# First attention of a Perceiver block: where the projection stands in TensorE's queue, a 28th ring slot, and who shifts the last scores

## The chip, the cores and the metric

The kernel runs on one core of one Trainium2 chip. The metric is device time in microseconds (us) of one execution, and the figure given is the median of several executions. Everything is fp32. The engines of the core are TensorE (PE in the profile, with PEld for its weight loads), VectorE (DVE), ScalarE (ACT), GpSimd (POOL) and SyncE (SP, which only issues transfers here). The program gives each engine its own queue of instructions.

## The reference

The model has two blocks. Each does cross-attention of 128 rows of x (256 wide) on a long context of 12,544 rows (192 wide), then self-attention, then a feed-forward part with experts. Only the first cross-attention is touched by the diff, apart from the size of a buffer ring that all stages share:

```python
q = (x @ Wq + bq).reshape(B, N, 16, 16)
k = (y @ Wk + bk).reshape(B, M, 16, 16)      # M = 12544
v = (y @ Wv + bv).reshape(B, M, 16, 16)
scores = jnp.einsum('bnhd,bmhd->bhnm', q, k) / sqrt(16)
attn = softmax(scores, axis=-1)
out = jnp.einsum('bhnm,bmhd->bnhd', attn, v)
h = relu(out @ W1 + b1)
x = x + (h @ W2 + b2)
```

The softmax runs over 12,544 keys, for 16 heads and 128 queries. The kernel does not hold all scores at once, so it works with maxima of parts of the keys and corrects for them at the end.

## The kernel before, in words

**Tiling.** The first attention handles the heads in two octets of eight. Within an octet it goes through the context in superblocks of 1024 keys (the last has 256), and a superblock is cut into groups of 256 keys. There are 49 groups per octet, 98 in all, and one step `t` of the main loop begins with one group. Ten groups in a row (or nine at the end of an octet) form a range. A range has its own maximum per query and head. There are ten ranges, which start at steps 0, 10, 20, 30, 40, 49, 59, 69, 79 and 89.

**A group's life.** `scores(t)` (TensorE, L411) writes the scores of a group into two PSUM tiles of two banks each, one for each k in 0, 1. `keep(t)` copies both tiles to two slots of an SBUF ring (ScalarE, L424) and folds them into a running maximum `mx` of the range (VectorE, L429). The copy of one tile goes on while the maximum of the other is taken. The pool has two buffers of that kind, so the next scores need both tiles to have been copied and compared. When the range has ended, `fold` halves `mx` (L436), `range_maximum` turns it with TensorE transposes (L250) and reduces it on VectorE (L446), and one step later `range_spread` spreads the negated maximum over all partitions with further transposes (L255) into two PSUM banks, one of the `w` kind and the bank `m`. `range_spread_out` copies them to SBUF (ScalarE, L466). Twelve steps after its scores, a group's slots get that value added: three quarters by GpSimd from SBUF (`shifted_gpsimd`) and one quarter by VectorE from the PSUM bank (`shifted_vector`), both on L476; from group 86 on it is half and half. Then ScalarE takes the exponentials (L486). One step later `attend` multiplies with v on TensorE (L499) into one bank `o` per range. At the end of the range `collected` and `gather` move the result to `accs`.

**The projection.** Keys and values are projected from the context on TensorE four steps ahead (`pieces(t + AHEAD)`, `AHEAD` is 4). A superblock has four pieces: the first half of the keys, the second half of the keys, the first half of the values and the second half of the values. A first half does the part of the contraction that is laid out in two row tiles (L214 for keys, L232 for values), for both of its PSUM banks, and then the whole part for the first bank (L217, L239). A second half does the whole part of the second bank. VectorE evacuates each bank (`keys_out` L372, `values_out` L376). Keys go to one of three `kT` buffers, values to one of `NV = 5` buffers `vs`. The first piece also issues the context loads for its superblock on SP (L198, L200).

**Buffers.** The ring has `RING = 27` slots of 128 x 1024. The first attention holds two slots per group for `LAG = 13` steps. The later stages use the same ring for weights and for the second attention's scores. [...]

**Order.** The order on every engine is written out by hand in a loop of `len(groups) + LAG + 1` steps, under `tc.manual_schedule()`. Within a step t, with `o = t - LAG` and `e = t - LAG + 1`, it goes: scores of t, spread, `attend(o)`, GpSimd's shifts of e, `keep(t)`, spread out, exponentials of e, VectorE's shifts of e + 1, fold and range maximum, collecting, the projection pieces, gathering.

**The second attention** has a similar loop of its own (scores L786, p*v L860, projection L214 to L239), and its copies to the ring are on L803, its sums on L883. Its order is not part of the diff.

Of the kernel before, what the change touches and what calls it, by code (L numbers as in the profile page):

```python
# [8 lines left out]
F32 = mybir.dt.float32  # L9
AF = mybir.ActivationFunctionType  # L10
ALU = mybir.AluOpType
AX = mybir.AxisListType

P = 128
# [4 lines left out]
NE = 8  # L19
KB = 512  # L20
SB = 1024
RING = 27
EPS = 1e-5


# [8 lines left out]
def perceiver(ctx: ExitStack, tc: tile.TileContext, a: dict, out: bass.AP):  # L34
    nc = tc.nc
# [17 lines left out]
    def ps_w(name):  # L53
        return banks["pool"].tile([P, KB], F32, tag="w", name=name, bufs=banks["w"])
# [36 lines left out]
    ident = const.tile([P, P], F32, name="ident")  # L91
# [154 lines left out]
    def turned(pt, src):  # L246

        m = src.shape[1]
        for i in range(m):
            nc.tensor.transpose(pt[:, i * P : (i + 1) * P], src[:, i, :], ident)  # L250
        return pt[:, : m * P].rearrange("p (m q) -> p m q", q=P)
# [52 lines left out]
    with tc.tile_pool(name="l0w", bufs=1) as lw:  # L304
# [4 lines left out]
        with psum_pool("ps0", 2) as pp, tc.tile_pool(name="l0x", bufs=1) as work:  # L309
# [3 lines left out]
            AHEAD, LAG = 4, 13  # L313
            NV = 5
# [5 lines left out]
            range_of, start_of = [], []  # L320
# [3 lines left out]
                range_of.append(len(start_of) - 1)  # L324
            last_of = [t for t in range(len(groups)) if last[t]]

            kTs, ps, mx, folded, spreads, kept, os, deferred = {}, {}, {}, {}, {}, {}, {}, {}
            vs = [work.tile([P, 8, 152], F32, name=f"x0_v{i}") for i in range(NV)]
            for v in vs:
                nc.gpsimd.memset(v, 1.0)  # L330
# [86 lines left out]
            def keep(t, st):  # L417

                b = range_of[t]
                ps[t] = [slot(f"x0_p{t}_{k}") for k in range(2)]  # L420
                if t == start_of[b] + 1:
                    mx[b] = work.tile([P, 2, 2, KB], F32, tag="mx", name=f"x0_mx{b}")
                for k in range(2):
                    nc.scalar.copy(ps[t][k], st[k].rearrange("p a n -> p (a n)"))  # L424
                    if first[t]:
                        continue
                    m = mx[b][:, 1 - k]
                    old = ps[t - 1][1 - k].rearrange("p (a n) -> p a n", a=2) if t == start_of[b] + 1 else m
                    nc.vector.tensor_tensor(m, st[1 - k], old, ALU.max)  # L429

            def fold(b):

                folded[b] = work.tile([P, 2, 2, 256], F32, tag="folded", name=f"x0_folded{b}")
                for k in (1, 0):
                    m = mx[b][:, k].rearrange("p a (c n) -> p a c n", c=2)
                    nc.vector.tensor_tensor(folded[b][:, k], m[:, :, 0], m[:, :, 1], ALU.max)  # L436

            def bank_m(name):
                return pp.tile([P, KB], F32, tag="m", name=name, bufs=1)

            def range_maximum(b):
                free = last_of[b] - LAG + 4 >= start_of[b]
                for k in (1, 0):
                    pt = bank_m(f"x0_mt{b}_1") if k and free else ps_w(f"x0_mt{b}_{k}")
                    pt = turned(pt, folded[b][:, k].rearrange("p a (u q) -> p (a u) q", q=P))
                    nc.vector.tensor_reduce(  # L446
                        negmax[:, b].rearrange("p (u i) -> p i u", u=2)[:, 2 * k : 2 * k + 2],
                        pt.rearrange("p (a u) q -> p a u q", u=2), AX.X, ALU.max, negate=True,
                    )

            def range_spread(b):

                pbs = [x.rearrange("p (a n) -> p a n", a=2) for x in (ps_w(f"x0_mb{b}"), bank_m(f"x0_m{b}"))]
                kept[b] = pbs[1]
                for k in range(2):
                    for i in range(2):
                        for u in range(2):
                            h = 4 * u + 2 * k + i
                            spread_column(pbs[k][:, i, u * P : (u + 1) * P], negmax[:, b, h : h + 1])
                return pbs  # L460
# [6 lines left out]

            def shares(t):

                return (2, 1) if t + LAG - 1 < len(groups) else (2, 0)  # L470

            def shift(engine, t, k, banks, by):
                if banks.stop > banks.start:
                    v = ps[t][k].rearrange("p (a c n) -> p a c n", a=2, c=2)[:, banks]
                    n = banks.stop - banks.start
                    engine.tensor_tensor(v, v, by[:, banks].unsqueeze(2).to_broadcast([P, n, 2, 256]), ALU.add)  # L476
# [3 lines left out]
                    shift(nc.gpsimd, t, k, slice(0, shares(t)[k]), spreads[range_of[t]][:, 2 * k :])  # L480

            def shifted_vector(t):
                shift(nc.vector, t, 1, slice(shares(t)[1], 2), kept[range_of[t]])

            def exponent(t, k):
                nc.scalar.activation(ps[t][k], ps[t][k], AF.Exp)  # L486
# [20 lines left out]
            def collected(b):  # L507
                oT = work.tile([P, 2, P], F32, tag="oT", name=f"x0_oT{b}", bufs=1)
                nc.vector.tensor_copy(oT.rearrange("p u q -> p (u q)"), os.pop(b)[:, 0:256])
                return oT  # L510

            def gather(b, oT):

                pt = turned(ps_w(f"x0_ot{b}"), oT)
                nc.vector.tensor_copy(
                    accs[:, b].rearrange("p (u i) d -> p u i d", u=2),
                    pt.rearrange("p u (i d) -> p u i d", i=4)[:, :, :, 0:17],
                )

            with tc.manual_schedule():  # L520
                for t in range(AHEAD):
                    for f in pieces(t):
                        f()
                oTs = {}
                for t in range(len(groups) + LAG + 1):
                    e, o = t - LAG + 1, t - LAG
                    e = e if 0 <= e < len(groups) else None
                    o = o if 0 <= o < len(groups) else None
                    st = scores(t) if t < len(groups) else None
                    b = range_of[t - 2] if 2 <= t < len(groups) + 2 and last[t - 2] else None  # L530
                    spread = range_spread(b) if b is not None else None
                    if o is not None:
                        attend(o)
                    if e is not None:
                        shifted_gpsimd(e)
                        if first[e]:
                            shifted_vector(e)
                    if t < len(groups):
                        keep(t, st)
                    if b is not None:  # L540
                        range_spread_out(b, spread)
                    if e is not None:
                        for k in range(2):
                            exponent(e, k)
                    if 0 <= t - LAG + 2 < len(groups) and not first[t - LAG + 2]:
                        shifted_vector(t - LAG + 2)
                    if 1 <= t < len(groups) + 1 and last[t - 1]:
                        fold(range_of[t - 1])
                        range_maximum(range_of[t - 1])
                    if o is not None and last[o]:  # L550
                        oTs[range_of[o]] = collected(range_of[o])
                    for f in pieces(t + AHEAD):
                        f()
                    if t > LAG and last[t - LAG - 1]:
                        b = range_of[t - LAG - 1]
                        gather(b, oTs.pop(b))

                nr = NR // 2
                acc = work.tile([P, 2, 8, 17], F32, name="x0_acc")
                allneg = small.tile([P, 2, 8], F32, tag="allneg", name="x0_allneg")  # L560
                by_octet = negmax.rearrange("p (j b) h -> p j b h", j=2)
                nc.vector.tensor_reduce(allneg, by_octet.rearrange("p j b h -> p j h b"), AX.X, ALU.min)
                fall = work.tile([P, 2, nr, 8], F32, name="x0_fall")
                nc.vector.tensor_tensor(
                    fall, allneg.unsqueeze(2).to_broadcast([P, 2, nr, 8]), by_octet, ALU.subtract
                )
                nc.scalar.activation(fall, fall, AF.Exp)
                nc.vector.tensor_tensor(
                    accs, accs, fall.rearrange("p j b h -> p (j b) h").unsqueeze(3).to_broadcast([P, NR, 8, 17]),
                    ALU.mult,  # L570
                )
                for j in range(2):
                    nc.vector.tensor_reduce(
                        acc[:, j].rearrange("p h d -> p (h d)"),
                        accs[:, j * nr : (j + 1) * nr].rearrange("p b h d -> p (h d) b"), AX.X, ALU.add,
                    )
# [560 lines left out]
```

## Time and profile before

| what | value |
|---|---|
| median of three executions | 1682.87 us |
| lowest and highest | 1678.96 and 1683.24 us |
| the profiled execution, in all | 1676.23 us |
| its span in the profile | 1674.5 us |
| its mean granted TensorE clock | 0.976 of full speed |
| busy in the span: PE, DVE, ACT, POOL | 1536.2, 1177.6, 985.2, 864.4 us |
| scores of step 0 begin at | 19.85 us |
| scores of step 97, the last, begin at | 471.06 us |
| the correction over the ranges begins at | 508.05 us |

The profile gives for each group of instructions its line, engine, operation and tiles, how long it was busy, and what ended the idle time before it. A timeline line reads: start in us, length in us, engine, line, operation, result and inputs, form, how many instructions are merged into the line, and in brackets the idle time before it with the instruction that ended it. A waits line reads: who waited for whom, the total in us, how many times, and the longest wait. A windows line gives, for a stretch of time, the busy time of each engine with its number of instructions, the granted clock, the share of the DMA engines and GB/s. The times in the profile are of one execution, so they are to be set against 1676.23 us and not against the median.

### The profile page before, as it was taken

How to read it: one execution, taken by the hardware profiler on the slowest of the kernel's cores; microseconds unless marked ns; L12 is line 12 of the kernel's file. 1: busy time of each engine (PE TensorE's matmuls, PEld its weight loads, DVE VectorE, ACT ScalarE, POOL GpSimd, SP SyncE). 2: the span in 40 equal slices, each digit the busy share in tenths (PEclk: the TensorE clock that was granted, in tenths of full speed). 3: DMA queues.
4: the chain of work that ended last, by engine and by line, in shares of the span. 5: the costliest groups of instructions: out<-in, count | busy, mean ns of one | idle time of the engine just before them, and what ended most of it. 6: DMA issues, size and time to landing. Idle time of an engine off the chain costs nothing.

```text
span 1674.5 us, 39737 instructions
## 1 busy us (share of the span) xinstructions
PE 1536.2 (92%) x17143; PEld 1169.9 (70%) x17143; DVE 1177.6 (70%) x1258; ACT 985.2 (59%) x1178; POOL 864.4 (52%) x554
## 2 busy tenths in 40 slices
PE   6899889998875897999999999999999999999978
PEld 4555555665544774578778778777788787777868
DVE  5777787777765323667777777687777777778952
ACT  3688878888882112566566566556566565665530
POOL 1477777777780000076386476575664763863000
PEclk9999999999997799999999999999999999999979
DMA  3111021111046306423223222232332222323950
GB/s 99 39 59 39 25 58 40 39 39 58 7 139 221 126 0 173 147 77 96 81 77 93 82 79 81 81 92 62 96 94 74 86 80 79 96 77 117 298 168 4
DMA packets 68420, 145.57 MB, mean 87 GB/s; under 512 B 8851, under 2 KB 27027, under 8 KB 68246
## 3 DMA queue, kind: packets, MB, share of 16 engines
q1 hardware_dynamic: 68246, 143.04, 28.3%
q8 instruction: 135, 2.21, 0.6%
q14 instruction: 39, 0.32, 0.1%
HBM read 142.87 MB, written 0.13 MB: 85 GB/s over the span
## 4 chain that ended last, share of the span: by engine, by line
PE 57%; DVE 10%; ACT 2%; issue 1%; POOL 1%; DVEq 0%; ACTq 0%
PE x_s L786 11%; PE x_k L217 10%; PE x_v L239 9%; PE x_o L860 8%; PE x_k L214 5%; PE x_v L232 4%; DVE x_part L883 2%; PE f_h L694 2%; PE f_py L704 2%; PE f_h L1073 2%; DVE x_sums L879 2%; DVE x_mx L810 1%; DVE x_p L841 1%; POOL x_p L476 1%; PE f_py L1082 1%
## 5 line engine op out<-in xcount | busy, mean ns | idle before, releaser
L841 POOL TENSOR_TENSOR x_p<-x_p,x_spread 128x1024 f32<-128x1024 f32 (+1 forms) x175 | 402.6, 2324 | 199.3 <-ACT x_spread L834 199.1
L476 POOL TENSOR_TENSOR x_p<-x_p,x_spread 128x1024 f32<-128x1024 f32 (+1 forms) x184 | 335.2, 1869 | 160.8 <-ACT x_spread L466 154.5
L883 DVE TENSOR_REDUCE x_part<-x_p 128x256 f32<-128x1024 f32 (+1 forms) x175 | 329.7, 1924 | 1.3 <-ACT x_p L849 1.3
L810 DVE TENSOR_TENSOR x_mx<-x_s,x_mx 128x1024 f32<-128x1024 f32 (+1 forms) x184 | 221.0, 1201 | 151.7 <-PE x_s L786 137.2
L803 ACT COPY x_p<-x_s 128x1024 f32<-128x1024 f32 (+1 forms) x200 | 199.1, 995 | 191.2 <-DVE x_mx L810 108.4
L888 POOL TENSOR_TENSOR x_sums<-x_sums,x_part 128x256 f32<-128x256 f32 x161 | 118.6, 736 | 307.1 <-DVE x_part L883 306.9
L424 ACT COPY x_p<-x_s 128x1024 f32<-128x1024 f32 x196 | 198.2, 1012 | 106.1 <-PE x_s L411 73.7
L239 PEld LDWEIGHTS x_v<-ywv_lo,x_ctx_lo 128*128 128x128 f32 x1568 | 189.3, 192 | 38.3 <-issue 36.8
L429 DVE TENSOR_TENSOR x_mx<-x_s,x_mx 128x1024 f32<-128x1024 f32 x156 | 187.0, 1221 | 39.4 <-PE x_s L411 22.6
L786 PE MATMUL x_s<-x_qT,x_kT 64*128 64x128 f32 x3136 | 203.1, 279 | 3.9 <-ACT x_p L803 3.9
L786 PEld LDWEIGHTS x_s<-x_qT,x_kT 64*128 64x128 f32 x3136 | 183.1, 188 | 28.2 <-issue 15.6
L849 ACT ACTIVATE x_p<-x_p 128x1024 f32<-128x1024 f32 (+1 forms) x200 | 197.8, 1037 | 1.4 <-DVE x_p L841 1.3
L486 ACT ACTIVATE x_p<-x_p 128x1024 f32<-128x1024 f32 x196 | 195.9, 1055 | 1.0 <-POOL x_p L476 1.0
L217 PE MATMUL x_k<-x_ctx_lo,ywk_lo 128*128 128x512 f32 (+1 forms) x412 | 194.2, 594 | 0.0
L860 PE MATMUL x_o<-x_p,x_v 128*64 128x128 f32 x3136 | 193.6, 276 | 0.0
L239 PE MATMUL x_v<-ywv_lo,x_ctx_lo 128*128 128x128 f32 x1568 | 193.1, 276 | 0.0
L860 PEld LDWEIGHTS x_o<-x_p,x_v 128*64 128x64 f32 x3136 | 169.6, 137 | 11.9 <-issue 1.1
L771 ACT COPY x_v<-x_v 128x512 f32<-128x512 f32 (+1 forms) x208 | 116.3, 562 | 78.4 <-PE x_v L239 77.7
L499 PE MATMUL x_o<-x_p,x_v 128*32 128x128 f32 x3136 | 129.6, 280 | 32.1 <-ACT x_p L486 31.1
L499 PEld LDWEIGHTS x_o<-x_p,x_v 128*32 128x32 f32 x3136 | 88.6, 111 | 77.2 <-ACT x_p L486 72.4
L232 PEld LDWEIGHTS x_v<-ywv_hi,x_ctx_hi 64*128 64x128 f32 x1568 | 107.6, 189 | 49.0 <-issue 25.2
L757 ACT COPY x_kT<-x_k 128x512 f32<-128x512 f32 (+1 forms) x104 | 58.2, 560 | 134.6 <-PE x_k L217 134.6
(237 smaller groups left out, 1705.0 us busy)
## 6 DMA issues: line engine op xcount, KB each, us to landing
x_ctx_lo<-in_ctxT_dram SPq DMA_DIRECT2D x131, 512.0 KB, 4.1
x_ctx_hi<-in_ctxT_dram SPq DMA_DIRECT2D x262, 128.0 KB, 4.0
f_w<-in_L_ffn_W_dram SPq DMA_DIRECT2D x32, 512.0 KB, 6.5
f_gating<-n_kernel_gating_EDF_dram SPq DMA_DIRECT2D x8, 512.0 KB, 7.2
f_up<-L_ffn_kernel_up_EDF_dram SPq DMA_DIRECT2D x8, 512.0 KB, 7.1
f_wd<-ffn_kernel_down_EFD_dram SPq DMA_DIRECT2D x8, 512.0 KB, 8.2
x_ctx_lo<-in_ctxT_dram SPq DMA_DIRECT2D x11, 128.0 KB, 2.1
xw<-in_L_xattn_W_dram SPq DMA_DIRECT2D x2, 512.0 KB, 3.9
```

The source lines that it names most:

```text
L217: nc.tensor.matmul(ps[r][:, :h], wk[0][:, js], lo[:, r * h : (r + 1) * h], start=False, stop=True)
L239: nc.tensor.matmul(ps[r][:, kc * P : (kc + 1) * P], lo[:, r * h + kc * P : r * h + (kc + 1) * P], wv[0][:, js], start=False, stop=True, sk ...
L424: nc.scalar.copy(ps[t][k], st[k].rearrange("p a n -> p (a n)"))
L476: engine.tensor_tensor(v, v, by[:, banks].unsqueeze(2).to_broadcast([P, n, 2, 256]), ALU.add)
L499: nc.tensor.matmul(os[b][32 * i : 32 * i + 32, u * P : (u + 1) * P], v[:, 2 * g + c, 17 * (2 * i + u) : 17 * (2 * i + u) + 32], p[i // 2][ ...
L786: nc.tensor.matmul(st[:, u, c * P : (c + 1) * P], kTs[t][rs, ks], qT[rs, j, :], start=True, stop=True)
L803: nc.scalar.copy(scores_kept(ps[t][i], sts[i].shape[2] // P), sts[i])
L810: nc.vector.tensor_tensor(mx[j][:, :, : n * P], sts[i], old, ALU.max)
L841: engine.tensor_tensor(v, v, spreads[j].unsqueeze(2).to_broadcast([P, 2, n, P]), ALU.add)
L849: nc.scalar.activation(v, v, AF.Exp)
L860: nc.tensor.matmul(o[us, 0:P], vs[t][:, c0 + c, us], p[:, n0 : n0 + P], start=(c0 + c == 0), stop=(c0 + c == total - 1), skip_group_check= ...
L883: nc.vector.tensor_reduce(part, v, AX.X, ALU.add)
```

## The change

The diff makes five edits, all in the first attention except for the size of the ring.

- The ring gets 28 slots. `fold` writes its result over the first half of `mx` and the tile `folded` goes; the transposes read `mx`.
- In the main loop the projection pieces are put between scores and `attend`. Where the piece belongs to a superblock with the same v buffer as the group that `attend` reads (`same`), `attend` stays ahead of it. That holds for each first half of keys, and for all steps from 45 to 61.
- `fold` comes ahead of VectorE's shift, and `range_maximum` comes at the end of a step, after `attend`. The spread of a range comes at step `max(l + 2, l0 + LAG - 2)` for a range from l0 to l, which is one step later than before for the two ranges of nine groups.
- In the first range the maxima are taken from the ring slots in SBUF after both copies, and not from the PSUM tiles.
- For the last range `shares` returns (1, 0): GpSimd shifts one quarter of a group and VectorE three quarters, from the two PSUM banks, both of which are kept.

```diff
-RING = 27
+RING = 28
...
                     m = mx[b][:, 1 - k]
                     old = ps[t - 1][1 - k].rearrange("p (a n) -> p a n", a=2) if t == start_of[b] + 1 else m
-                    nc.vector.tensor_tensor(m, st[1 - k], old, ALU.max)
+                    if b:
+                        nc.vector.tensor_tensor(m, st[1 - k], old, ALU.max)
+                if b == 0 and not first[t]:
+
+                    for k in range(2):
+                        m = mx[b][:, k]
+                        new, old = (ps[i][k].rearrange("p (a n) -> p a n", a=2) for i in (t, t - 1))
+                        nc.vector.tensor_tensor(m, new, old if t == 1 else m, ALU.max)
 
             def fold(b):
 
-                folded[b] = work.tile([P, 2, 2, 256], F32, tag="folded", name=f"x0_folded{b}")
                 for k in (1, 0):
                     m = mx[b][:, k].rearrange("p a (c n) -> p a c n", c=2)
-                    nc.vector.tensor_tensor(folded[b][:, k], m[:, :, 0], m[:, :, 1], ALU.max)
+                    nc.vector.tensor_tensor(m[:, :, 0], m[:, :, 0], m[:, :, 1], ALU.max)
...
             def range_maximum(b):
-                free = last_of[b] - LAG + 4 >= start_of[b]
                 for k in (1, 0):
+
+                    free = last_of[b] + 1 - LAG + 2 >= start_of[b] - 1
                     pt = bank_m(f"x0_mt{b}_1") if k and free else ps_w(f"x0_mt{b}_{k}")
-                    pt = turned(pt, folded[b][:, k].rearrange("p a (u q) -> p (a u) q", q=P))
+                    for a in range(2):
+                        for u in range(2):
+                            n0 = (2 * a + u) * P
+                            nc.tensor.transpose(pt[:, n0 : n0 + P], mx[b][:, k, a, u * P : (u + 1) * P], ident)
...
-                kept[b] = pbs[1]
+                kept[b] = pbs
...
             def shares(t):
 
+                if range_of[t] == NR - 1:
+                    return 1, 0
                 return (2, 1) if t + LAG - 1 < len(groups) else (2, 0)
...
             def shifted_vector(t):
-                shift(nc.vector, t, 1, slice(shares(t)[1], 2), kept[range_of[t]])
+                for k in range(2):
+                    shift(nc.vector, t, k, slice(shares(t)[k], 2), kept[range_of[t]][k])
...
+                spread_at = {max(l + 2, l0 + LAG - 2): b for b, (l0, l) in enumerate(zip(start_of, last_of))}
                 for t in range(len(groups) + LAG + 1):
...
                     st = scores(t) if t < len(groups) else None
-                    b = range_of[t - 2] if 2 <= t < len(groups) + 2 and last[t - 2] else None
+                    ended = range_of[t - 1] if 1 <= t < len(groups) + 1 and last[t - 1] else None
+                    b = spread_at.get(t)
                     spread = range_spread(b) if b is not None else None
-                    if o is not None:
-                        attend(o)
...
+                    if ended is not None:
+                        fold(ended)
                     if 0 <= t - LAG + 2 < len(groups) and not first[t - LAG + 2]:
                         shifted_vector(t - LAG + 2)
-                    if 1 <= t < len(groups) + 1 and last[t - 1]:
-                        fold(range_of[t - 1])
-                        range_maximum(range_of[t - 1])
-                    if o is not None and last[o]:
-                        oTs[range_of[o]] = collected(range_of[o])
-                    for f in pieces(t + AHEAD):
+                    ahead = pieces(t + AHEAD)
+
+                    same = o is not None and ahead and groups[t + AHEAD][0] % NV == groups[o][0] % NV
+                    for f in () if same else ahead:
                         f()
+                    if o is not None:
+                        attend(o)
+                        if last[o]:
+                            oTs[range_of[o]] = collected(range_of[o])
+                    for f in ahead if same else ():
+                        f()
+                    if ended is not None:
+                        range_maximum(ended)
```

## The prediction

> **What bounds the kernel now.** I read the page's slices first, then a table of windows, one row per range, then the timeline inside a range, then the waits. The windows table separates two worlds:
>
> ```profile
> core 0: us, PE busy (x) PEld busy (x) DVE busy (x) ACT busy (x) POOL busy (x), PEclk, DMA share, GB/s
> ...
> 100.81:147.68 46.87, 42.68 (x586) 26.83 (x587) 37.32 (x45) 39.50 (x43) 34.99 (x20) 1.00 0.18 52
> ...
> 471.06:507.83 36.77, 26.31 (x484) 18.09 (x484) 20.51 (x23) 29.80 (x32) 26.35 (x12) 0.91 0.62 207
> ...
> 640.00:1660.00 1020.00, 988.50 (x10607) 788.86 (x10608) 747.94 (x713) 572.47 (x738) 522.04 (x343) 0.99 0.34 100
> ```
>
> The last row, mostly the second attention, is TensorE from end to end (988.5 of 1020), and its order is not touched. The first row is steps 20 to 29 of the first attention: no engine is full, so waits set its 46.87 us. The second row is the drain. A step of the first attention looks like this:
>
> ```profile
> 83.15 1.15 PE L411 MATMUL x_s<-x_qz,x_kT 32*128 32x256 f32 x16 [0.21 <-ACT x_p L424]
> ...
> 84.22 0.41 PE L499 MATMUL x_o<-x_p,x_v 128*32 128x128 f32 x4
> ...
> 85.05 1.07 PE L499 MATMUL x_o<-x_p,x_v 128*32 128x128 f32 x28 [0.41 <-ACT x_p L486]
> ...
> 86.04 1.13 PE L214 MATMUL x_k<-x_ctx_hi,xwk_hi 64*128 64x512 f32 x4
> ...
> 87.10 1.13 PE L217 MATMUL x_k<-x_ctx_lo,xwk_lo 128*128 128x512 f32 x2
> ...
> 88.16 1.15 PE L411 MATMUL x_s<-x_qz,x_kT 32*128 32x256 f32 x16
> ```
>
> Scores take 1.07 us, then p*v waits in TensorE's queue for the exponentials of the step before (84.22 to 85.05), and the projection stands behind it, though it needs none of them. ScalarE in turn starts its copy only after the next scores. The starts of the scores give the step lengths: 5.02 us when the projection is a first half (heavy, 2.12 to 2.18 us), 3.64 when it is a second half (light, 1.06), and 7.05, 4.16 and 6.00 in the three steps in which a range ends (100.81, 107.86, 112.02, 118.02). The waits name the same:
>
> ```profile
> PE x_o L499 <- ACT x_p L486: 31.1, 64, 1.9
> ...
> ACT x_p L424 <- PE x_o L499: 11.2, 8, 4.2
> ```
>
> The second is the ring: with 27 slots the second copy of a step needs the slot that this step's p*v frees.
>
> [...] the fold takes 0.68 us, but where GpSimd was busy one of the pair took 2.89:
>
> ```profile
> 239.92 3.49 DVE L436 TENSOR_TENSOR x_folded<-x_mx 128x512 f32<-128x512 f32 x2
> ...
> 238.64 3.62 POOL L476 TENSOR_TENSOR x_p<-x_p,x_spread 128x1024 f32<-128x1024 f32 x2
> ```
>
> [...] Here the second copy waits for the first maximum (15.1 us in 44 waits of L424).
>
> **The change part by part.** No matmul is added or removed; TensorE's queue per step goes from scores, p*v, projection to scores, projection, p*v. Where the key projection's superblock uses the v buffer that p*v still reads, `same` keeps the old order: every first half of keys, and all of steps 45 to 61.
>
> *Value-heavy steps.* Scores 1.07 + projection 2.18 + p*v 1.01 = 4.26 us in place of 5.08; the exponentials end some 1.9 us after the scores start (85.05 - 83.15), under the projection. Behind it VectorE must free the second projection bank; its evacuation ends about 4.7 us after the light step's scores start, 1.1 after the heavy step's: no wait to speak of. Key-heavy steps stay at 5.04, and light ones at 3.65: copy at 1.24, second copy 1.34 later behind the first maximum, next scores 1.07 after that. Four steps: 17.37 before, 4.26 + 3.65 + 5.04 + 3.65 = 16.60 after.
>
> *End of a range* (three steps). The transposes move behind p*v, so the projection no longer stands behind the reduction that frees its bank (0.72 of wait), and the ring's extra slot takes the copy off p*v (1.01). First step, key-heavy: 1.07 + 0.83 of wait + 1.0 + 2.12, then 1.25 for the transposes, whose second half waits for an evacuation: 6.29; value-heavy 1.07 + 2.18 + 1.01 + 1.06: 5.32. Second: 4.18 (scores 1.07, spread 1.02, light projection 1.09, p*v 1.0). Third: 4.26 or, key-heavy, 5.25. Both kinds sum to 14.7 for 17.2.
>
> *Whole ranges.* Steps 20 to 29: 14.72 + 3.65 + 5.04 + 3.65 + 4.26 + 3.65 + 5.04 + 3.65 = 43.7 for 46.87. Steps 30 to 39: 42.9, and 0.2 for the fold, for 46.94. Range by range, us saved: 13 to 19 2.6 (1.5 of it in step 13, where the projection covers the table load); 20 to 39 7.0; 40 to 48 2.5; 49 to 52 4.3 (25.88 becomes some 21.6, since the spread moves a step later and no longer waits for bank m, 2.6 us on TensorE); 53 to 61 1.7; 62 to 68 1.6; 69 to 88 7.2; 89 to 97 2.9. Together 29.8.
>
> *First range.* Its copies no longer wait for a maximum (3.59 us a step becomes 3.24 in light steps), but the maxima start after the copies, so the evacuation is 0.9 later and a heavy step's second bank waits: 4.11 for values, 3.56 for keys. Mean 3.54. GpSimd is idle there (57.36 us before its first shift)[...]. 1.0 saved with steps 10 to 12; 2 saved to 1 lost as bounds, by the unseen SBUF maximum.
>
> *Fold in place* adds no instruction. The next range's first maximum must wait for the transposes, but comes after scores that are behind them in TensorE's queue: nothing. Folding earlier against GpSimd is the new cost: GpSimd works 35.7 us from a spread (112.69 to 148.41), and the next fold comes at 34.1 for 36.7 now. It waits 1.6 us, with shift and evacuation queued behind; the transposes need them only after projection and p*v, so 0 to 0.2 of it shows.
>
> *Drain.* Before, GpSimd paces it at 2.33 us a group, ScalarE waiting for it:
>
> ```profile
> 482.62 21.06 POOL L476 TENSOR_TENSOR x_p<-x_p,x_spread 128x1024 f32<-128x1024 f32 x9 [6.26 <-PE x_mb L255]
> ...
> 503.71 2.00 ACT L486 ACTIVATE x_p<-x_p 128x1024 f32<-128x1024 f32 x2 [0.32 <-POOL x_p L476]
> ```
>
> After, GpSimd does one 1.26 us half, VectorE 0.6 + 1.14[...], and ScalarE's two exponentials, 1.91, are the bound. It starts level with before: spread out 12.4 us after the last scores, then ten groups, 31.5, for 34.7. Less about 1.0, because the last fold meets GpSimd: 2.0 saved, bounds 0.5 and 3.2.
>
> *Queues moved past.* SP's context loads go with the key-heavy projection; a buffer is refilled one superblock ahead (some 17 us) against 4.1 us to land: 0. The second attention gets the 28th slot too: ScalarE's wait for L883 there (17.8 us, 13 times) lies beside a full TensorE. I take 0, bounds 0 and -3.
>
> Sum: 29.8 + 1.0 + 2.0 = 32.8, say 32. The profiled execution, span 1674.5 and 1676.2 in all, becomes 1644; it lies 6.6 under the median of the runs, 1682.9, which becomes **1651**.
>
> **Rivals.**
> (a) [...] If TensorE gets faster, every fold waits for GpSimd's end, and period = 36.9 + about 7.5 from fold to spread = 44.4 for my 43.3. For: the 2.89 us fold. Against: the slack above. Eight ranges lose 1: 1659.
> (b) *Only ends and drain gain:* the heavy step stays at 5.0, because ScalarE and not TensorE's order holds it. Against: ScalarE is idle 7 us of a range. Saved: 7 ends x 2.5 - 2 = about 15: 1668.
> (c) *ScalarE alone bounds:* 3.9 us a step over 85 steps with 1 us per range is 341 for 405 less TensorE's `same` steps: some 45 saved, 1638.
> (d) *Slower:* projection ahead of p*v makes TensorE wait for VectorE. Place: the second bank of L232, whose evacuation stands behind two maxima and a shift. The gain is spread over some 16 value-heavy steps, so from 2 us of wait in each it is gone; at 2.5 it loses 40 against the 33 of the sum, near 1690. VectorE is busy 37.3 of 46.9, which speaks against it.
> (e) *The order does nothing* because `same` holds too often: it holds in one step of four outside 45 to 61; no more than 1680.
>
> **How the numbers follow.** My forecast 0.58 (1644 to 1658), (a) 0.16, (b) 0.08, (c) 0.08, (d) 0.07, (e) 0.03. The range 1637 to 1667 takes the first, (a) and (c), and the bounds of first range, drain and slot. A change under 0.3% (5 us) can't be told from none: faster 0.90, same 0.03, slower 0.07.
>
> **What would show it.** Right: value-heavy steps near 4.3 and light ones near 3.65 between starts of scores, range ends near 14.7, a range 43 to 44; p*v's wait for exponentials about halved; drain exponentials back to back at 0.96; folds of 2 us and more. Wrong: L232 waiting for L376 or L372 by more than 1 us a step, steps 0 to 9 longer than 35.6, or the second attention moved by more than 3.

## The result and the profile after

The changed kernel takes 1651.6 us, median of four executions (1650.5 to 1656.4), beside 1681.2 for the kernel before on the same chip (1679.0 to 1683.2). The ratio is 0.983, 95% interval 0.9805 to 0.9855. A later comparison on another chip gave 1653.7 and the same 0.983 (0.9803 to 0.9857). It is faster by about 30 us; the forecast was 1651.

The windows below are those of the profile before: steps 20 to 29, the drain, and mostly the second attention. The columns are the same.

```profile
core 0: us, PE busy (x) PEld busy (x) DVE busy (x) ACT busy (x) POOL busy (x), PEclk, DMA share, GB/s
...
102.91:146.98 44.07, 41.13 (x586) 26.70 (x586) 38.12 (x45) 38.88 (x43) 35.73 (x21) 1.00 0.18 54
...
453.00:487.18 34.18, 24.57 (x484) 17.26 (x484) 27.95 (x35) 29.37 (x32) 17.75 (x12) 0.95 0.70 229
...
620.00:1640.00 1020.00, 990.42 (x10611) 790.32 (x10611) 747.82 (x714) 572.46 (x738) 524.73 (x343) 0.99 0.34 100
```

Steps 20 to 29 do the same 586 matmuls in 44.07 us instead of 46.87; TensorE is now busy for 41.13 of them. In the drain GpSimd has 17.75 us of work in place of 26.35, VectorE 27.95 in place of 20.51. The last row hardly differs; what it hides is told under the square.

The TensorE timeline of a value-heavy step, from scores to scores:

```profile
130.26 1.16 PE L411 MATMUL x_s<-x_qz,x_kT 32*128 32x256 f32 x16 [0.41 <-ACT x_p L424]
131.35 1.35 PE L232 MATMUL x_v<-xwv_hi,x_ctx_hi 64*128 64x128 f32 x16
132.63 1.16 PE L239 MATMUL x_v<-xwv_lo,x_ctx_lo 128*128 128x128 f32 x8
133.72 1.08 PE L512 MATMUL x_o<-x_p,x_v 128*32 128x128 f32 x32
134.73 1.14 PE L411 MATMUL x_s<-x_qz,x_kT 32*128 32x256 f32 x15
```

From 130.26 to 134.73 no bracket appears: projection has filled the place of the wait, and p*v runs as one block of 32. The step is 4.47 us, TensorE alone. In the waits, p*v for the exponentials (now L512 for L499) has gone from 31.1 us in 64 to this:

```profile
PE x_o L512 <- ACT x_p L499: 18.0, 39, 1.7
```

The copies' wait for p*v, 11.2 us before, has no line any more. And the ScalarE timeline of the drain is one line:

```profile
465.20 19.05 ACT L499 ACTIVATE x_p<-x_p 128x1024 f32<-128x1024 f32 x20
```

Twenty exponentials back to back at 0.95 us, with no wait for GpSimd between them.

Two places of the first attention are not as forecast. At the fold in step 49, in the timelines of VectorE, GpSimd and TensorE:

```profile
233.07 5.01 DVE L442 TENSOR_TENSOR x_mx<-x_mx 128x512 f32<-128x512 f32 x2
238.01 0.68 DVE L488 TENSOR_TENSOR x_p<-x_p,x_m 128x512 f32<-128x512 f32 x1
238.61 0.74 DVE L372 TENSOR_SCALAR x_kT<-x_k,cols 128x512 f32<-128x512 f32 x1
```
```profile
226.20 10.73 POOL L488 TENSOR_TENSOR x_p<-x_p,x_spread 128x1024 f32<-128x1024 f32 x6
```
```profile
239.40 0.66 PE L455 MATMUL x_mt<-ident,x_mx 128*128 128x128 f32 x4 [2.34 <-DVE x_kT L372]
240.84 1.12 PE L455 MATMUL x_mt<-ident,x_mx 128*128 128x128 f32 x4 [0.79 <-DVE x_negmax L456]
241.89 2.09 PE L411 MATMUL x_s<-x_qz,x_kT 32*128 32x256 f32 x16
243.91 1.94 PE L512 MATMUL x_o<-x_p,x_v 128*32 128x128 f32 x32
```

GpSimd's shifts end at 226.20 + 10.73 = 236.93, and VectorE's folds, which began at 233.07, end at 238.08: one of the two took 4.4 us instead of 0.68. TensorE stands 2.34 us, and then scores take 2.09 us for 1.15 and p*v 1.94 for 1.08. That is a lower clock, which a window shows (after the busy times comes PEclk, 0.53):

```profile
241.89:247.45 5.56, 5.56 (x51) 3.11 (x50) 3.64 (x4) 3.07 (x4) 0.00 (x0) 0.53 0.02 4
```

The other place is the first range, here a heavy step of it on TensorE:

```profile
43.17 1.13 PE L411 MATMUL x_s<-x_qz,x_kT 32*128 32x256 f32 x12 [0.21 <-ACT x_p L424]
44.24 0.49 PE L232 MATMUL x_v<-xwv_hi,x_ctx_hi 64*128 64x128 f32 x2
45.31 1.77 PE L232 MATMUL x_v<-xwv_hi,x_ctx_hi 64*128 64x128 f32 x14 [0.59 <-DVE x_kT L372]
47.02 2.07 PE L239 MATMUL x_v<-xwv_lo,x_ctx_lo 128*128 128x128 f32 x8
```

The second bank of the projection waits for the evacuation behind both new maxima, in each value-heavy step; in a key-heavy one L214 takes 2.14 us, which is 1.13 without such a wait. In this step the clock also fell (14 matmuls take 1.16 us in the other value-heavy steps; PEclk 0.75 over the step).

By stage, from the starts of scores, in us. Column A is the profile set against the forecast (1656.36 us in all, the slowest of its four), B that of the second comparison (1653.48). The correction begins, as in the table of before, with the reduction that makes `allneg` (508.05 before, 486.59 in A):

| stage | forecast saved | before | after A | saved A | saved B |
|---|---|---|---|---|---|
| start to first scores | 0 | 19.85 | 22.00 | -2.2 | -0.9 |
| steps 0 to 12 | 1.0 | 48.40 | 50.65 | -2.3 | -0.7 |
| 13 to 19 | 2.6 | 32.56 | 30.26 | 2.3 | 2.3 |
| 20 to 39 | 7.0 | 93.81 | 87.60 | 6.2 | 6.2 |
| 40 to 48 | 2.5 | 43.63 | 41.47 | 2.2 | 2.2 |
| 49 to 52 | 4.3 | 25.88 | 25.43 | 0.5 | 0.5 |
| 53 to 68 | 3.3 | 74.24 | 71.80 | 2.4 | 2.4 |
| 69 to 88 | 7.2 | 94.09 | 87.60 | 6.5 | 6.5 |
| 89 to 96 | 2.9 | 38.60 | 36.19 | 2.4 | 2.4 |
| last scores to the correction | 2.0 | 36.99 | 33.59 | 3.4 | 3.4 |
| correction to end | 0 | 1166.47 | 1167.71 | -1.2 | -1.2 |
| sum | 32.8 | | | 20.2 | 23.1 |

The start to the first scores varies from 19.85 to 22.00 us among all profiles of the study, so its row says nothing of the change. The traces show 20 to 23 us, the medians 30. The profiled execution of before, 1676.23, lies below every one of its timed executions in this study (1676.4 to 1686.8), and A above its median. Part of this is TensorE's clock from the correction to the end, in order before, A and the keys-first kernel that the experiments add (each stretch in the times of its own profile):

```profile
508.05:1674.52 1166.47, 1102.48 (x11255) 885.77 (x11255) 796.66 (x807) 594.08 (x763) 522.16 (x344) 0.97 0.33 100
```
```profile
486.59:1654.30 1167.71, 1109.24 (x11255) 891.51 (x11255) 795.88 (x807) 594.08 (x763) 524.86 (x344) 0.96 0.34 100
```
```profile
477.19:1640.53 1163.34, 1102.20 (x11255) 885.55 (x11255) 795.63 (x807) 594.05 (x763) 524.91 (x344) 0.97 0.33 100
```

Each has 11,255 matmuls there. The clock records of the traces sum to 69 us at half clock in before and in the keys-first profile, and to 85 in A and B. A's code from there on is that of the keys-first kernel, and takes 4.4 us longer. So I estimate that before, with the clock of A and B, would have taken some 4 us more in its profile, which brings the saving in the traces to 25 to 28. The timed executions of before agree in direction: those under 1677 us have a mean granted clock of 0.976 to 0.978, those over 1684 one of 0.970 to 0.974. What else differs inside them no trace here shows.

### The profile page after: what moved, and what is told of

Its sections match the earlier page's. It is cut to its first block, busy times and chain, and to the rows that moved or that the text cites. A ratio compares the mean times of both kernels' runs of the same rounds, so it can differ in the third digit from the quotient of the medians.

```text
span 1654.3 us, 39758 instructions
## 1 busy us (share of the span) xinstructions
PE 1540.8 (93%) x17143; PEld 1177.7 (71%) x17143; DVE 1188.2 (72%) x1267; ACT 979.5 (59%) x1178; POOL 857.6 (52%) x554
## 4 chain that ended last, share of the span: by engine, by line
PE 76%; DVE 13%; ACT 8%; issue 2%; DMA 1%; POOLq 0%; ACTq 0%; DVEq 0%; SPq 0%
PE x_k L217 13%; PE x_v L239 11%; PE x_s L808 11%; PE x_o L882 10%; PE x_v L232 6%; PE x_k L214 6%; PE x_s L411 4%; DVE x_mx L430 3%; ACT x_p L424 3%; ACT x_p L499 3%; PE x_o L512 3%; PE f_h L716 2%; PE f_h L1095 2%; PE f_py L726 2%; DVE x_part L905 1%
## 5 line engine op out<-in xcount | busy, mean ns | idle before, releaser
L863 POOL TENSOR_TENSOR x_p<-x_p,x_spread 128x1024 f32<-128x1024 f32 (+1 forms) x175 | 402.8, 2326 | 201.2 <-ACT x_spread L856 201.1
L488 POOL TENSOR_TENSOR x_p<-x_p,x_spread 128x512 f32<-128x512 f32 (+1 forms) x184 | 325.6, 1816 | 142.6 <-ACT x_spread L476 70.1
L424 ACT COPY x_p<-x_s 128x1024 f32<-128x1024 f32 x196 | 193.4, 1015 | 93.2 <-PE x_s L411 78.6
L499 ACT ACTIVATE x_p<-x_p 128x1024 f32<-128x1024 f32 x196 | 196.3, 1062 | 0.4 <-DVE x_p L488 0.4
L430 DVE TENSOR_TENSOR x_mx<-x_s,x_mx 128x1024 f32<-128x1024 f32 x140 | 168.1, 1221 | 31.6 <-PE x_s L411 16.8
L232 PEld LDWEIGHTS x_v<-ywv_hi,x_ctx_hi 64*128 64x128 f32 x1568 | 107.3, 189 | 49.3 <-issue 25.0
L512 PE MATMUL x_o<-x_p,x_v 128*32 128x128 f32 x3136 | 122.0, 279 | 18.9 <-ACT x_p L499 18.0
L411 PE MATMUL x_s<-x_qz,x_kT 32*128 32x256 f32 x1568 | 119.0, 403 | 15.9 <-ACT x_p L424 15.6
```

What stands on the lines that cost most here:

```text
L232: nc.tensor.matmul(ps[r][:, ks], hi[rs, ks], wv[1][rs, js], start=(kc == 0), stop=False, skip_group_check=True,)
L863: engine.tensor_tensor(v, v, spreads[j].unsqueeze(2).to_broadcast([P, 2, n, P]), ALU.add)
```

## The experiments

**The square of order and slot.** Three kernels: the changed one with TensorE's order put back, with the ring put back, and with both.

```diff
-                    same = o is not None and ahead and groups[t + AHEAD][0] % NV == groups[o][0] % NV
+                    same = True
```

> The changed kernel with TensorE's old order in every step (p*v ahead of the projection); slot, maxima, fold, transposes and drain stay changed. My theory (the order is worth 0.5 to 0.7 us in each of 16 value-heavy steps, 1.5 in step 13, and some at range ends): value-heavy steps return from about 4.5 to 5.0, steps 20 to 39 from 87.6 to about 90, and the time is 1664 (1660 to 1668). Rival 'the order is worth nothing, slot, ends and drain carry the gain': 1651 within 3, value-heavy steps still near 4.5. Rival 'the order is all of it': above 1672.

Measured 1662.0 us (1659.9 to 1664.1), ratio to before 0.9884 (0.9865 to 0.9904), whose interval lies clear of the changed kernel's. Value-heavy steps are back at 5.07 or 5.08 and ranges of ten steps at 45.5. Steps 49 to 52 went the other way, 22.2 for 25.4: TensorE there waits 1.45 us for the fold and keeps its clock (its next scores take 1.15 us). By stages the order saves 10.7 us in steps 13 to 48 and 53 to 96 and gives 3.2 back by the way it meets the fold at step 49; the medians have 8 to 10 for the whole.

```diff
-RING = 28
+RING = 27
```

> The changed kernel with 27 ring slots instead of 28, the order of TensorE kept new. My theory (the second copy of a step then waits for p*v, which now stands behind the projection): in heavy steps ScalarE's second copy ends near 5.2 us after the scores instead of 2.4, the exponentials follow it, and steps grow by 0.5 to 1.5 us each; 1651 + 16 x 1 + 19 x 0.3 = about 1673 (1660 to 1690), and L424 waiting for p*v (L512) comes back as the largest of its waits. Rival 'the slot was only worth the 11 us of the old wait': 1651 to 1656. The second attention within 1 us either way.

Measured 1701.2 us (1699.1 to 1702.5): slower than before, ratio 1.0113 (1.0088 to 1.0139). The mechanism is the expected one, the loss is over twice my number (48 to 50 for 22), since light steps suffer too. In its waits and on ScalarE:

```profile
ACT x_p L424 <- PE x_o L512: 56.2, 51, 2.0
```
```profile
181.18 1.00 ACT L424 COPY x_p<-x_s 128x1024 f32<-128x1024 f32 x1
183.83 1.01 ACT L424 COPY x_p<-x_s 128x1024 f32<-128x1024 f32 x1 [1.65 <-PE x_o L512]
184.74 2.01 ACT L499 ACTIVATE x_p<-x_p 128x1024 f32<-128x1024 f32 x2
```

The second copy of value-heavy step 34 starts at 183.83, 0.08 after the end of p*v's block, and exponentials, the next scores and their maxima follow it down the line; light steps grow from 3.62 to as much as 5.28. The experiment holds its own control: from 45 to 58, where `same` keeps the old order, light and value-heavy steps stay at 3.64 and 5.08.

The second attention was expected within 1 us, and is not. Between the starts of its scores 20 and 90, counted from 0, it takes 630.5 us here and 630.9 before, and 627.7 to 627.8 in each of the ten profiles with 28 slots: the slot saves 2.8 us there, 0.5 at each of the six ends of a pass over the keys. With 27 slots ScalarE's copy waits for the sums that free a slot, here and before:

```profile
ACT x_p L825 <- DVE x_part L905: 17.4, 13, 1.5
```
```profile
ACT x_p L803 <- DVE x_part L883: 17.8, 13, 1.8
```

With 28 this line is gone. At the first of the six ends, with 27 slots, the chain is: ScalarE waits 1.48 us for the sums and copies until 851.73, VectorE stands 0.53 us for that copy and then takes the maximum, the fold and the evacuation (L781), and TensorE stands for that. Its transposes there, with 27 slots and in A:

```profile
855.06 0.44 PE L250 MATMUL x_mt<-ident,x_folded 128*128 128x128 f32 x2 [0.71 <-DVE x_kT L781]
```
```profile
811.34 0.44 PE L250 MATMUL x_mt<-ident,x_folded 128*128 128x128 f32 x2 [0.23 <-DVE x_kT L781]
```

The stage table does not show it, since A and B ran longer at half clock after the correction. The keys-first profile, with the clock of before, is 3.1 us shorter there than before.

> The changed kernel with 27 slots and with TensorE's old order (p*v ahead of the projection); it closes the square of slot and order. With 28 slots the order is worth 10.4 us (1662.0 to 1651.6 or 1653.7), with the new order the slot is worth 48 (1701.2 to 1653.7). My theory (with p*v first, the slot comes free before ScalarE asks for it in all steps but those in which a range ends, where the kernel before waited 11.2 us in all): the slot is worth 8 to 12 here, 1672 (1669 to 1675); the order with 27 slots is then a loss of about 29. Rival 'the slot matters as much in the old order': above 1690.

Measured 1674.1 us (1669.7 to 1678.4), ratio 0.9961 (0.9946 to 0.9976); copies wait for p*v for 8.5 us in nine places. The square, in us:

| | p*v first | projection first |
|---|---|---|
| 27 slots | 1674.1 | 1701.2 |
| 28 slots | 1662.0 | 1651.6 and 1653.7 |

The slot is worth 12 with the old order and 48 to 50 with the new one, each with some 3 in the second attention. The order costs 27 with 27 slots and gains 8 to 10 with 28. A group is copied in step t and read by p*v in step t + 13: fourteen groups in flight, two slots each, are 28. With 27, a step's second copy must wait for the p*v of the same step, which the new order puts off by the length of the projection. The upper left cell also says what the other edits bring with neither: 7.5. By stages the drain has 3.2 of it (33.74 us for 36.99) and steps 13 to 96 have 5.8, while steps 0 to 12 lose. Fold, transposes and the later spread were not put back one by one, so how they share the 5.8 is open.

**The drain's shares put back.**

```diff
-                if range_of[t] == NR - 1:
-                    return 1, 0
```

> The changed kernel with the drain's shifts shared as before (GpSimd two banks of the first block and, until the last groups, one of the second). My theory (GpSimd's two banks, 2.33 us a group, pace the drain, and in the changed kernel ScalarE at 1.91 us does): from the last scores to the correction of the accumulators 34.5 us become 36.5 to 37.5, the rest unchanged, 1654 (1652.5 to 1655.5). Rival 'the drain is shorter only because the range ends earlier relative to GpSimd': 1651 to 1652.

Measured 1656.5 us (1654.8 to 1659.6), 2.8 more than the changed kernel beside it, with ranges that overlap; the stage tells them apart, from last scores to the correction 37.1 for 33.6. ScalarE's timeline shows GpSimd's pace again, one line like this for each group, 2.33 us apart:

```profile
474.09 2.01 ACT L497 ACTIVATE x_p<-x_p 128x1024 f32<-128x1024 f32 x2 [0.33 <-POOL x_p L486]
```

All steps ahead of it are as in A to within 0.02 us.

**The first range's maxima from PSUM.**

```diff
-                    if b:
-                        nc.vector.tensor_tensor(m, st[1 - k], old, ALU.max)
-                if b == 0 and not first[t]:
+                    nc.vector.tensor_tensor(m, st[1 - k], old, ALU.max)
+                if False:
```

> The changed kernel with the first range's maxima taken from the PSUM scores again, as all other ranges do. My theory (the SBUF maxima start after both copies and push the evacuations of the projection behind them, so that a heavy step's second bank waits): heavy steps in 0 to 9 go from 5.1 to about 4.2, steps 0 to 9 from 36.6 to about 35.3, steps 10 to 12 from 14.0 to about 13; time 1649 (1647 to 1651). Rival, as the edit was priced in the prediction (copies freed of the maxima are worth 1.0): 1652.5, steps 0 to 9 longer than 36.6.

Measured 1649.4 us (1647.1 to 1650.8), which touches the range of the changed kernel; the stages are clearer. Steps 0 to 9 take 35.53, steps 10 to 12 12.12, in all 47.65 for 50.65 in A and 49.11 in B. The shape is not quite the one expected: there are no heavy and light steps any more, each takes 3.59. With maxima from SBUF a light step is 2.24 and a heavy one 5.1 to 5.2; nine and ten together take 8.99 where these take 8.43. So the edit costs 1.5 us in B, at full clock there, and 1.5 more in A, with its stretch at half clock (PEclk 0.75 over step 6). This kernel has no such stretch here. Of the eight profiles with maxima from SBUF, B alone has none in steps 0 to 12; five have one, and the two with 27 slots have two (steps 2 and 10).

**Keys first.** `same` is asked only where the projection makes values.

```diff
-                    same = o is not None and ahead and groups[t + AHEAD][0] % NV == groups[o][0] % NV
+                    same = o is not None and t + AHEAD < len(groups) and (groups[t + AHEAD][1] >= 2 or sbs[groups[t + AHEAD][0]][1] == NS - 1) and groups[t + AHEAD][0] % NV == groups[o][0] % NV
```

> The changed kernel with the old order kept only where the projection makes values (which is where a v buffer could still be read); the 19 steps with a first half of keys whose order was kept for that reason now put the projection ahead of p*v too. My theory (the wait of p*v for the exponentials holds them at 5.01): they fall to 4.4 to 4.5, 0.5 x 19 = 10 us less, 1641 (1638 to 1645). Rival 'ScalarE or the evacuations pace a block of four steps': less than 3 us, the light steps give back what the heavy ones win, 1649 to 1652.

Measured 1643.6 us (1639.2 to 1645.7), ratio 0.9771 (0.9749 to 0.9794): 8 to 10 under the changed kernel by the medians, 7.2 by the stages from step 13 to 96. Key-heavy steps in the middle of a range fall from 5.01 to between 4.34 and 4.55, and the light ones stay at 3.62. Steps 30 to 39 gain little (43.08 for 43.53): step 30 goes from 5.50 to 6.47. The pair of folds takes 3.48 us there for 2.34 in A, and TensorE's transposes wait 0.74 us for the VectorE instruction behind it, which they do not in A. I take the fold for the cause, as TensorE is sooner and GpSimd is not.

**GpSimd relieved ahead of the fold.** VectorE takes one bank more of the last two groups of each range, four in the ranges 30 to 39 and 79 to 88.

```diff
+                if t + (4 if range_of[t] in (3, 8) else 2) > last_of[range_of[t]]:
+                    return 2, 0
                 return (2, 1) if t + LAG - 1 < len(groups) else (2, 0)
```

> The changed kernel with GpSimd's part of the last two groups of each range cut from three banks to two (of the last four groups in the two ranges that come before a range of nine groups); VectorE shifts the third bank. GpSimd then ends its shifts of a range 2.5 us (5 us) sooner. My theory (the folds of VectorE wait for GpSimd to go idle, which is what steps 49 to 52 lost): all folds near 0.68, step 49 falls from 9.9 to about 7, steps 49 to 52 to about 22.5, drain 0.5 to 1 shorter, 1647.5 (1645 to 1650). Rival 'the slow step 49 is TensorE's own (low clock, transposes and table of waits), the fold lies beside it': folds at 0.68 but the time within 1.5 of 1651. Rival 'VectorE is the next bound': ranges longer by 0.5 each, 1654 or more.

Measured 1650.4 us (1649.5 to 1652.4), 1.2 to 3.3 under the two medians of the changed kernel where 3.5 was expected; the totals alone don't tell the two apart. The stages can. No fold takes over 0.79 us, and at step 49:

```profile
225.82 4.75 POOL L490 TENSOR_TENSOR x_p<-x_p,x_spread 128x1024 f32<-128x1024 f32 x2
```
```profile
232.16 1.28 DVE L442 TENSOR_TENSOR x_mx<-x_mx 128x512 f32<-128x512 f32 x2
```
```profile
236.46 0.66 PE L455 MATMUL x_mt<-ident,x_mx 128*128 128x128 f32 x4 [0.84 <-DVE x_kT L372]
237.90 0.66 PE L455 MATMUL x_mt<-ident,x_mx 128*128 128x128 f32 x4 [0.79 <-DVE x_negmax L456]
238.49 1.15 PE L411 MATMUL x_s<-x_qz,x_kT 32*128 32x256 f32 x16
```

GpSimd is done at 230.57, the fold takes 1.28 for two, TensorE waits 0.84 and keeps its clock. Step 49 is 7.96 for 9.91, step 50 3.62 for 5.56, steps 49 to 52 22.0 for 25.4. What was given back: steps 30 and 79 take 6.03 for 5.50, as VectorE's longer shift (1.21 for 0.68) stands ahead of the evacuation (L372) that TensorE waits for in L232.

**The three together.** Keys first, maxima from PSUM, and a relief of four groups that keeps out of the last ones of a range.

```diff
+                if range_of[t] in (3, 8) and 3 < last_of[range_of[t]] - t < 8:
+                    return 2, 0
```

> Three edits together on the changed kernel: projection of keys ahead of p*v everywhere, the first range's maxima from PSUM, and GpSimd relieved of one bank in four groups in the middle of the two ranges that come before a range of nine groups (not in the last groups of a range, where the longer VectorE shift cost 0.5 us of steps 30 and 79). If they add: 8 + 2.2 + about 3 less than 1651, that is 1638 (1636 to 1640), steps 0 to 12 at 47.7, 49 to 52 near 22.3. Rival 'TensorE reaches the fold sooner, so this relief is too small': 49 to 52 near 24, 1641.

Measured 1642.5 us (1637.1 to 1643.9): not 1638. Steps 0 to 12 are 47.66 and 49 to 52 20.05, as hoped or better, but step 44 takes 7.74 for 6.24 and step 45 6.56 for 4.20. Step 44 projects the short superblock, keys and values together:

```profile
206.65 0.71 PE L217 MATMUL x_k<-x_ctx_lo,xwk_lo 128*128 128x128 f32 x4
208.94 1.05 PE L232 MATMUL x_v<-xwv_hi,x_ctx_hi 64*128 64x128 f32 x4 [1.58 <-DVE x_kT L372]
209.92 1.22 PE L239 MATMUL x_v<-xwv_lo,x_ctx_lo 128*128 128x128 f32 x4
211.07 2.09 PE L411 MATMUL x_s<-x_qz,x_kT 32*128 32x256 f32 x16
```

The relief fell on the one step in which VectorE had no room. Moved to the groups that VectorE shifts in steps 46 to 48 and 95 to 97:

```diff
-                if range_of[t] in (3, 8) and 3 < last_of[range_of[t]] - t < 8:
+                if range_of[t] in (3, 8) and 1 < last_of[range_of[t]] - t < 5:
```

> As the combined kernel, with GpSimd's relief moved from the groups shifted in steps 43 to 46 (92 to 95) to those shifted in steps 46 to 48 (95 to 97), three groups instead of four. My theory (the combined kernel lost 3.9 us in steps 44 and 45 and 1.1 in 93 and 94 because the longer VectorE shift stood ahead of the evacuations of the short superblock, TensorE waited 1.6 us and then ran at half clock): step 44 back to 6.2, 45 to 4.2, 93 to 6.2, and steps 49 to 52 stay near 20 to 22; time 1638 (1636 to 1640.5). Rival 'three groups are too few, the fold waits again': 49 to 52 at 24 or more, 1641 or more.

Measured 1637.9 us (1635.3 to 1639.4), ratio 0.9740 (0.9715 to 0.9765). Steps 44 and 45 are 6.23 and 4.20, 49 to 52 20.6. This is the fastest kernel of the study, 14 to 16 us under the changed one. Without any relief:

> As the combined kernel without any relief of GpSimd: projection of keys first, first range's maxima from PSUM. If the relief is worth what steps 49 to 52 lost to the fold's wait: 3 us slower than the kernel with the later relief, 1641 (1639 to 1643), with one fold above 4 us and steps 49 to 52 at 25.4. Rival 'that wait is hidden once the order is new everywhere': the two within 1 us.

Measured 1642.3 us (1638.8 to 1643.9), on the same chip as the one ahead. Steps 49 to 52 take 24.16 and the fold's pair 5.04; TensorE waits 3.02 us. All other stages from step 0 to the correction agree with the relieved kernel's to within 0.05. The relief is worth 4.4 by the medians and 3.6 by the stage.

**The changed kernel again.**

> The changed kernel itself once more, for a comparison on the same chip: 1651 (1649 to 1653), and in its profile one stretch of TensorE at half clock in steps 0 to 12 and one in step 50, as all runs so far with both of its causes had.

Measured 1653.7 us (1649.9 to 1656.0). The half clock in step 50 is there; in steps 0 to 12 it is not, contrary to what I wrote: it comes in seven of the eight profiles with that range's maxima from SBUF.

## Why the prediction was right, and where it was not

**Right for the reason given: steady steps.** The wait that was named, p*v for the exponentials with the projection behind it, is gone from value-heavy steps. They take 4.47 to 4.68 (4.79 in step 14) and not 4.26: the term that was too small is the projection, 2.37 us where a middle row of before gave 2.18. Light steps are 3.62 for 3.65, ends of ranges 14.76 and 14.88 for 14.7. So the six stages from step 13 to 96, without 49 to 52, saved 22.0 of the 25.5 forecast. Putting the order back took 10.7 of it away.

**Priced too low: the slot.** The prediction gave the 28th slot the 1.01 us of wait at each range end, and nothing in the second attention. The first is near what it is worth there with the old order (12 in all, some 3 of it in the second attention). It did not say that the new order depends on it; the square shows that the order loses 27 without it.

**The step that failed most: 49 to 52, 4.3 forecast, 0.5 measured.** The working said of the fold that it "waits 1.6 us" and that "0 to 0.2 of it shows". That was worked out for ranges of ten. Where the range that ends has nine groups, GpSimd still has the ten of the range ahead of it to shift, and the fold follows their spread by seven steps (42 to 49) and not eight: the fold waited 3.7 us, TensorE 2.34, and then lost about 2 more at half clock, which no part of the working had. (Before, step 50 ran in part at half clock too, PEclk 0.82, after a stop of 2.58 us.) The relief experiments show it: with GpSimd done ahead of the fold the stage takes 22.0, near the 21.6 that the prediction had, while everything else in it stands. Rival (a) named this wait, but as the pace of all ranges; it is one place. In steps 69 and 79 the first fold of a pair also waits, 0.7 and 1.1 us, but the steps are no shorter (6.52 and 6.03 for 6.52 and 5.49) where GpSimd was relieved and it takes 0.68.

**The other failed term: the first range, 1.0 forecast.** A maximum from SBUF, unseen when the term was worked out, takes 1.22 us (L436 in A), as one from PSUM does (L430), and the wait of the second bank was foreseen. The sizes were wrong: a heavy step was put at 4.11 or 3.56 with light steps at 3.24 and takes 5.1 to 5.2 with 2.24. At full clock steps 0 to 9 still come to 35.09 for the forecast 35.4; what fails there is steps 10 to 12, which the term had 0.8 shorter than before and which take 14.02 for 12.85. Step 10 alone is 6.74 for 5.56: it still carries both maxima of step 9 ahead of its evacuation, and with maxima from PSUM it takes 4.84. The measured effect is -0.7 in B, and -2.3 in A with its stretch at half clock. A sign named as "wrong" did appear, steps 0 to 9 of 36.63 in A; in B they are 35.09.

**The drain:** 3.4 for 2.0, by the mechanism told; put back, it costs 3.5. The 1.0 that was taken off for the last fold is what was wrong: that fold does wait 1.3 us for GpSimd, but in the kernel with the later relief it does not, and the drain there is 33.58 all the same.

**The second attention:** 0 forecast, about 3 saved, at the edge of the stated bounds and of the sign named as "wrong". The step that failed is that ScalarE's wait for L883 lies beside a full TensorE: with 27 slots TensorE stands 0.5 us longer for it at each end of a pass.

**Rivals.** (b), ends and drain alone, is out: with the order put back 8 to 10 us are lost. (c), ScalarE alone, is out for this kernel; keys first shows that there was room left, as key-heavy steps fall when they are not held by `same`. (d) had the right shape and the wrong wait: projection ahead of p*v does make the kernel slower, not through the second bank of L232 but through the ring, and only without the extra slot. (e) is out.

**The median.** The prediction put the changed kernel's profiled execution at 1644 and added 6.6, by which the profiled execution of before lay under its median. B is 1653.5 in its profiled execution, 0.2 under its median. So the forecast for a profile was 9.5 short, the offset of 6.6 belonged to that one execution of before, some 4 of it by its clock after the correction (the estimate above), and the two errors nearly cancel. That the forecast met the medians to within 3 us is partly luck.

## What to carry to other kernels

Before work is moved ahead of an instruction, list what that instruction sets free: here p*v frees a ring slot, and the same reordering costs 27 us with 27 slots and brings 8 to 10 with 28. A ring that stages share is to be looked at in each of them: the slot also saved 2.8 us in a stage that the prediction had left out. A wait that is harmless at the mean range has to be worked out again at the shortest one, and a relief put where the engine that takes the work has room: the one of four shifts gave back in steps 44, 45, 93 and 94 all that it won in 49 to 52, the one of three kept it. When a forecast's total is met, go through it by stages all the same.

## What the runs showed of the hardware

One fold took longer than any single instruction of GpSimd beside it. Those are 1.27 to 2.37 us and followed each other from 226.20 to 236.93; the fold, begun at 233.07, ended at 237.49, 0.56 after the last, with two of them begun meanwhile. VectorE's maxima and shifts, which read PSUM banks, took 1.21 to 1.23 and 0.68 us beside the same instructions. With GpSimd idle the pair of folds took 1.28 us.

TensorE's clock was at half after some short stops. Stops of 1.58, 2.34 and 3.02 us were followed by scores of 2.09 us for 1.15, while 0.84 and 1.45 at the same fold were not; in the first range a stop of 0.59 in each value-heavy step was followed by half clock at least once in seven of eight profiles. So the length of one stop does not tell the cases apart. In the clock records of before and A the half clock comes in stretches of 3.41 us or whole multiples of it, up to 27.31 (but for the last of each trace), and the longest of these stops did not bring the longest stretch: 3.41 us after 3.02 (PEclk 0.65 over step 50), 6.83 after 2.34. At step 49 the stop of 2.34 us costs about as much again at half clock (step 50 is 5.56 for 3.62). What adds up to the drop was not tried.
